# A mixture-of-experts layer hands its results to the next layer: rows scattered by token, or blocks written by slot and gathered by token

## The chip, the cores and the metric

The kernel runs on one core of one Trainium2 chip. The core has five engines that run their own instruction streams in order and meet at semaphores: PE (TensorE, the matrix multiplier; PEld is its weight load), DVE (VectorE), ACT (ScalarE), POOL (GpSimd) and SP (SyncE, which here only issues transfers). Sixteen DMA engines move data between main memory and the on-chip memories. SBUF is the working memory, with 128 partitions; PSUM takes the matmuls' results.

The metric is device time in microseconds (us) of one execution. Eight runs of the kernel before have a median of 2263.39 us, from 2252.53 to 2265.82.

## What is computed

The input x has 4 x 1024 tokens of 128 values. Six layers follow, each with a layer norm in front and added to x. What matters here is the third, the second mixture, and the fourth behind it.

```
x = x + 0.5 * moe(layernorm(x))        # 8 experts, 2 per token
x = x + mamba(layernorm(x))            # scan over time
x = x + 0.5 * moe(layernorm(x))        # the same weights: the "second mixture"
x = x + 0.5 * soft_moe(layernorm(x))   # 64 experts x 32 slots
x = x + gla(layernorm(x))              # gated linear attention
x = x + 0.5 * soft_moe(layernorm(x))
```

The mixture, cut to what matters (T = 4096 tokens, E = 8, K = 2, each expert has cap = 1024 slots):

```python
gates_k, idx_k = top_k(softmax(xt @ wg), K); gates_k /= gates_k.sum(-1)
loc   = position of the choice among all choices of its expert
valid = loc < cap
disp[idx_k, loc] = xt                       # tokens to slots
out   = relu(disp @ w1 + b1) @ w2 + b2      # per expert
y     = sum over k of gates_k * valid * out[idx_k, loc]   # slots back to tokens
```

The soft mixture takes logits = x @ phi.T + phi_b, a softmax over the 32 slots of each expert for the dispatch (its weighted sums over all tokens, X_tilde, are normalised and go through one matrix per expert), and a softmax over the 64 experts for the way back.

## The kernel before

The 4096 tokens are 32 tiles of 128; x stays in SBUF for the whole kernel (P = 128, NT = 32, D = 128). The 8192 slots of the mixture are NSB = 64 blocks of 128 (NSLOT = 8192).

**Routing, `slots`.** From the router's masks it works out each choice's slot (L307 to L320; a choice that finds its expert full gets a gate of 0). A one-hot matmul inverts this: for every slot the row of its token, in `src` (L373), and the row of its choice among the K x T = 8192 choices, in `dest` (L372). An empty slot gets a spare row of its own behind them (L364 to L366). `mamba_layer` comes in front of it, and the framework orders what lies between.

**Experts, `moe_experts`.** A loop over 16 blocks of 512 slots, with the order on PE, DVE, ACT and POOL as written by hand. Per block: four gathers by `src` on POOL (L402), each of 128 rows of 512 bytes from the normalised x in main memory; four transposes (L420) into dT (L422); eight passes for the hidden layer (L430, ACT's relu L434); 32 passes for the output (L444); `eo` = output + b2 on DVE (L449). Then four scatters by `dest` on POOL (L408) write eo's rows into `y2_d`, one row for each choice. Gathers run four blocks ahead in 20 buffers; eo has four buffers. In the last blocks, where there is nothing to gather, a small memset (L472) stands between scatters.

**Back to tokens, `combine`.** `bring` reads y2_d for four tiles in two plain transfers on SP (L488). `pieces` scales the first choice by its gate on ACT (L499), scales the second and adds x on DVE (L491), adds both (L509), and takes the layer norm's sums (L122, L123, L126 in `ln_sums` and `ln_eps`), root on POOL (L136) and shift on DVE (L143). It is a generator: each `yield` ends what one step of its user takes.

**First soft layer, `soft_bounded`.** It runs in the branch that was taken (`bounded`). Again the order on the four engines is written by hand. The dispatch loop has NK = 64 steps, two for each tile of tokens. Step k emits, in this order:

- one yield of `pieces` (eight of them make a group of four tiles),
- `logits(k)`: four passes (L980), and the minimum of the negated logits on DVE (L984); `expo(k)`: the exponential on ACT (L989),
- in the first four of each eight steps, `norm`: one tile of the next group, normalised on ACT (L198); in the fifth `turn` and `take`: four transposes (L966) and their copy to xT (L971). `turn` takes one of the two PSUM buffers that the logits use,
- `total(k-1)`: sums (L996) and reciprocal (L997) on DVE; `weigh(k-1)`: the product on POOL (L1001),
- `spread(k-3)`: four passes (L1012).

In front of the loop stand the pieces of the first group, its norm and turn, and the pieces of the second group. Before that, POOL sets rows of xT to 1 (L946). Behind the dispatch come the experts' part and the way back, which use the 14 buffers of the pool `lp` for their tiles L.

Of the kernel before, what the change touches and what calls it, by code (L numbers as in the profile page):

```python
# [69 lines left out]
def macaron_kernel(ctx: ExitStack, tc: tile.TileContext, a: dict, out: bass.AP):  # L70
# [132 lines left out]
    def moe_routes(tag, tp):  # L203
# [92 lines left out]
        def slots(src, dest, gate):  # L296
            with ExitStack() as s1:
# [31 lines left out]
                )  # L329
                hl_i = sp.tile([P, 2, C], I32, name="hl_i")  # L330
# [33 lines left out]
                none = sp.tile([P, NSB], F32, name="none")  # L364
                nc.vector.tensor_scalar(none, inv[:, 1, :], 0.0, None, ALU.is_equal)
                nc.vector.tensor_tensor(none, none, spare, ALU.mult)  # L366
# [5 lines left out]
                nc.vector.scalar_tensor_tensor(dest, row, -1.0, none, ALU.add, ALU.add)  # L372
                nc.vector.tensor_scalar(src, dest, T - 1, None, ALU.bitwise_and)  # L373
# [15 lines left out]
    def moe_experts(w1, w2, b2, tag, xn_d, src, dest):  # L389

        with ExitStack() as s1:
# [6 lines left out]
            spacer = wk.tile([P, 1], F32, name="spacer")  # L398

# [56 lines left out]
            with tc.manual_schedule(engines=ENGINES):  # L456
                for c in range(AHEAD * 4):
                    gather(c)
                turn(0)
                turn(1)  # L460
                hidden(0)
                for blk in range(NBLK + 1):
                    if blk + 2 < NBLK:
                        turn(blk + 2)
                    if blk + 1 < NBLK:
                        hidden(blk + 1)
                    for i in range(4):
                        c = (blk + AHEAD) * 4 + i
                        if c < NSB:
                            gather(c)  # L470
                        elif blk > 0:
                            nc.gpsimd.memset(spacer, 0.0)  # L472
                        if blk > 0:
                            scatter((blk - 1) * 4 + i)
                    if blk < NBLK:
                        output(blk)

    def combine(gate, ln, n=2, tag=None):
# [47 lines left out]
        return bring, pieces  # L526

# [394 lines left out]
    def soft_bounded(phiN, phiM, pbc, ew, eb, tag, ln, first=None, rest=None, after=None, last=False, yp=None):  # L922
# [12 lines left out]
        with ExitStack() as s:  # L935
# [223 lines left out]
            with tc.manual_schedule(engines=ENGINES):  # L1159
                if first:  # L1160
                    bring, pieces = first
                    bring(0, yp)
                    bring(4, yp)
                    run(pieces(0, yp))
# [4 lines left out]
                if first:  # L1169
                    run(pieces(4, yp))  # L1170
                else:
                    pieces = rest
                others = (_ for j in range(8, NT, 4) for _ in pieces(j, yp))
                for k in range(NK + CS * NB + XL + 3):
                    next(others, None)
                    if k < NK:
                        logits(k)
                        expo(k)
                        g, r = divmod(k, 8)
                        if 4 * (g + 1) < NT:  # L1180
                            if r < 4:
                                norm(4 * (g + 1) + r)
                            elif r == 4:
                                turn(g + 1)
                                take(g + 1)
                        elif r == 4:
                            maxima(0, NT - 4)
# [11 lines left out]
                    if 0 <= k - 1 < NK:  # L1199
                        total(k - 1)  # L1200
                        weigh(k - 1)
                    if 0 <= k - LAG < NK:
                        spread(k - LAG)
# [473 lines left out]
    dest = const.tile([P, NSB], I32, name="dest")  # L1677
    for j in range(0, NT, 4):
        ln_group(lns[0], j)

    with tc.tile_pool(name="moewa", bufs=1) as wpool:
        weights = moe_weights(wpool)
        with tc.tile_pool(name="rtmpa", bufs=1) as tp:
            route = moe_routes("a", tp)
            with (
                tc.tile_pool(name="rxa", bufs=4) as xp,
                tc.tile_pool(name="rpsa", bufs=2, space=PSUM) as ps,
            ):
                for j in range(0, NT, 4):
                    run(route.tiles(j, lns[0], nc.scalar, xp, ps))  # L1690
                    if j % 8 == 4:
                        route.top_two(j - 4, 8)
            route.slots(src, dest, gates[0])
        moe_experts(*weights, "a", route.xn_d, src, dest)
# [3 lines left out]
    with tc.tile_pool(name="rtmpb", bufs=1, side="right") as tp:  # L1698
# [5 lines left out]
        route.slots(src, dest, gates[1])  # L1704
# [12 lines left out]
    moe_experts(*weights, "b", route.xn_d, src, dest)  # L1717
    wpool.close()

    def behind_soft(soft):  # L1720
        gla_layer(lns[4], lns[5])
        ln_root(lns[5], 0, 8)
        soft("b", lns[5], rest=lambda j, _: ln_pieces(lns[5], j), last=True)
# [5 lines left out]
    with tc.If(bounded > 0) as cmp:  # L1729
        def soft(*a_, **k_):  # L1730
            soft_bounded(phiN, phiM, pbc, ew, eb, *a_, **k_)
        with tc.tile_pool(name="yb", bufs=2) as yp:
            soft("a", lns[3], combine(gates[1], lns[3]), after=after, yp=yp)
        behind_soft(soft)
    with cmp.Else():
        def soft(*a_, **k_):
            rest = k_.pop("rest", None)
            if rest:
                for j in range(8, NT, 4):
                    run(rest(j, None))  # L1740
            soft_layer(phiN, ew, eb, *a_, **k_)
        nc.scalar.activation(phiN, phiN, AF.Copy, scale=-1.0)
        with tc.tile_pool(name="yc", bufs=2) as yp:
            bring, pieces = combine(gates[1], lns[3])
            bring(0, yp)
            bring(4, yp)
            for j in range(0, NT, 4):
                run(pieces(j, yp))
# [75 lines left out]
```

## Time and profile before

The profiled execution took 2262.53 us, with a span of 2260.8 us; the mean granted clock of PE was 0.931.

| stretch, us from the span's start | length | PE busy | DVE | ACT | POOL | granted PE clock |
|---|---|---|---|---|---|---|
| experts of the second mixture, 881 to 1052 | 171.0 | 128.6 | 22.4 | 45.9 | 127.1 | 0.92 |
| dispatch, start, 1062 to 1075 | 13.0 | 9.6 | 8.7 | 7.6 | 1.1 | 0.71 |
| dispatch, eight steps, 1132.2 to 1160.8 | 28.6 | 26.9 | 24.4 | 10.9 | 16.6 | 1.00 |
| dispatch of the second soft layer, eight steps, 1839.3 to 1867.8 | 28.5 | 28.1 | 24.0 | 10.9 | 16.2 | 1.00 |

Each row is one stretch of the windows view: how long each engine was busy in it. The busy times of engines overlap, and a busy engine need not be the one that sets the end. The second soft layer has no pieces of a mixture, only those of its layer norm.

From the page's groups:

```profile
L1001 POOL TENSOR_TENSOR dm<-ex,sm 128x1024 f32<-128x1024 f32 x128 | 247.4, 1933 | 217.4 <-DVE sm L997 110.0
L408 POOL DMA_INDIRECT y_d<-eo,dest x128 | 125.7, 982 | 42.3 <-issue 25.0
```

A group's line gives line, engine and operation, the tiles written and read, shapes and count; then the busy time in us and the mean of one in ns; then how long the engine was idle just before them, and what ended most of it. L408 counts both mixtures, 64 scatters in each.

### The profile page before, as it was taken

To read this page: it belongs to the slowest core of one execution; us is meant where nothing else is said; L and a number is where in the kernel's file an instruction comes from. 1 tells how busy PE (TensorE), PEld (TensorE's weight loads), DVE (VectorE), ACT (ScalarE), POOL (GpSimd) and SP (SyncE) were. 2 spreads that over 40 slices of the span, in tenths; PEclk is the share of its full clock that TensorE was granted. 3 is DMA by queue.
4 is the path that set the end of the run, shared out by engine and by line. 5 is a ranking of instruction groups with operands and counts; after the bars stand their busy time and mean duration, and the time that the engine had idled before them with its cause. 6 is when DMAs were issued, how large, how long until landed. Compare 5 with 4: busy or idle time off the path is not lost. (4 is left out here: it accounts for less than half of the span.)

```text
span 2260.8 us, 18041 instructions
## 1 busy us (share of the span) xinstructions
PE 1913.5 (85%) x5889; PEld 890.4 (39%) x5889; DVE 1400.4 (62%) x1852; ACT 957.4 (42%) x1613; POOL 1407.3 (62%) x923
## 2 busy tenths in 40 slices
PE   5688668888888773975999989998888899989998
PEld 3466323333333232653344444443232344434443
DVE  4411578887788864112888745555877788744444
ACT  3222376677766642322334333332543333333331
POOL 2677368888888874676555556663444455556663
PEclk9999779999999895998999999999987899999999
DMA  7111333223223315112000000000000000000000
GB/s 252 32 52 51 111 122 116 99 102 118 100 91 120 102 39 201 46 52 70 19 19 0 1 1 1 0 0 6 0 1 0 1 0 1 0 1 5 10 10 15
DMA packets 63678, 111.23 MB, mean 49 GB/s; under 512 B 8000, under 2 KB 41424, under 8 KB 58582
## 3 DMA queue, kind: packets, MB, share of 16 engines
q1 hardware_dynamic: 49286, 83.46, 11.0%
q0 software_dynamic: 8192, 16.79, 2.5%
q10 hardware_dynamic: 6098, 9.75, 1.3%
q8 instruction: 48, 0.79, 0.1%
q14 instruction: 54, 0.43, 0.1%
HBM read 90.53 MB, written 19.44 MB: 49 GB/s over the span
## 5 line engine op out<-in xcount | busy, mean ns | idle before, releaser
L1001 POOL TENSOR_TENSOR dm<-ex,sm 128x1024 f32<-128x1024 f32 x128 | 247.4, 1933 | 217.4 <-DVE sm L997 110.0
L748 POOL TENSOR_TENSOR hc<-hst,Cs 128x1024 f32<-128x1024 f32 x128 | 292.5, 2294 | 53.5 <-DVE hst L732 29.2
L763 PE MATMUL py<-hc,ident 128*128 128x512 f32 x512 | 275.6, 666 | 49.3 <-POOL hc L748 49.3
L1109 POOL TENSOR_TENSOR acc<-acc,L 128x1024 f32<-128x1024 f32 x96 | 225.9, 2353 | 116.0 <-ACT L L1101 115.3
L1101 ACT ACTIVATE L<-pl,pbc 128x512 f32<-128x512 f32 x256 | 161.9, 683 | 284.2 <-PE pl L1091 273.7
L989 ACT ACTIVATE ex<-l,nmh 128x1024 f32<-128x1024 f32 x128 | 142.6, 1114 | 291.8 <-DVE nmh L984 274.6
L980 PE MATMUL l<-phiT,xT 128*128 128x512 f32 x512 | 248.3, 610 | 19.6 <-ACT ex L989 16.3
L1091 PE MATMUL pl<-xT,phiM 128*128 128x512 f32 x512 | 243.5, 600 | 0.1
L1012 PE MATMUL px<-dm,xn 128*128 128x512 f32 x512 | 241.4, 594 | 1.1 <-POOL dm L1001 1.1
L1135 PE MATMUL py<-L,yt 128*128 128x512 f32 x512 | 238.4, 593 | 4.4 <-DVE L L1125 4.4
L722 ACT ACTIVATE dA<-delta,A 128x512 f32<-128x512 f32 x256 | 177.3, 719 | 69.0 <-DVE hst L732 64.0
L984 DVE TENSOR_REDUCE nmh<-l 128x1 f32<-128x1024 f32 x128 | 156.1, 1220 | 80.6 <-PE l L980 80.0
L434 ACT ACTIVATE hT<-ph,cols 128x512 f32<-128x512 f32 x128 | 87.9, 687 | 217.9 <-PE ph L430 217.9
L763 PEld LDWEIGHTS py<-hc,ident 128*128 128x128 f32 x512 | 94.4, 200 | 197.9 <-issue 106.8
L714 POOL TENSOR_TENSOR dBu<-du,Bs 128x1024 f32<-128x1024 f32 x80 | 170.6, 2134 | 0.5 <-DVE nmr L143 0.5
L732 DVE TENSOR_TENSOR_SCAN hst<-dA,carry,dBu 128x512 f32<-128x512 f32 x128 | 155.5, 1264 | 23.9 <-POOL dBu L714 19.6
L732 DVE TENSOR_TENSOR_SCAN hst<-dA,dBu 128x512 f32<-128x512 f32 x128 | 147.6, 1204 | 24.4 <-POOL dBu L714 18.6
L980 PEld LDWEIGHTS l<-phiT,xT 128*128 128x128 f32 x512 | 97.8, 194 | 151.3 <-issue 116.9
L996 DVE TENSOR_REDUCE sm<-ex 128x32 f32<-128x1024 f32 x128 | 154.6, 1208 | 0.0
L408 POOL DMA_INDIRECT y_d<-eo,dest x128 | 125.7, 982 | 42.3 <-issue 25.0
L1125 DVE TENSOR_TENSOR L<-L,rd 128x1024 f32<-128x1024 f32 x128 | 147.1, 1212 | 0.1
L1135 PEld LDWEIGHTS py<-L,yt 128*128 128x128 f32 x512 | 96.8, 190 | 127.3 <-issue 116.9
(258 smaller groups left out, 2895.6 us busy)
## 6 DMA issues: line engine op xcount, KB each, us to landing
Cs<-bc_d SPq DMA_DIRECT2D x32, 1024.0 KB, 4.7
Bs<-bc_d SPq DMA_DIRECT2D x80, 256.0 KB, 3.1
w<-in_w SPq DMA_DIRECT2D x4, 2048.0 KB
y<-y_d SPq DMA_DIRECT2D x32, 256.0 KB, 2.9
y_d<-zero SPq DMA_DIRECT2D x1, 4096.0 KB
ew<-in_ew ACTq DMA_DIRECT2D x1, 4096.0 KB
x<-in_x SPq DMA_DIRECT2D x8, 256.0 KB, 8.1
xn_da<-xr ACTq DMA_DIRECT2D x8, 256.0 KB, 13.5
```

The costliest lines, as they stand in the source:

```text
L714: eng.tensor_tensor(dBu, r["du"], r.pop(("B", n)).unsqueeze(2).to_broadcast([P, HB, NC]), ALU.mult,)
L722: nc.scalar.activation(dA, r["delta"][:, :, c], AF.Exp, scale=A[:, c * DS + n : c * DS + n + 1],)
L732: nc.vector.tensor_tensor_scan(hst[:, :, c], r.pop(("dA", n, c)), dBu[:, :, c], 0.0 if h == 0 else carry[b][:, c, n : n + 1], ALU.mult, AL ...
L748: nc.gpsimd.tensor_tensor(hc, r.pop(("h", n)), Cs.unsqueeze(2).to_broadcast([P, HB, NC]), ALU.mult)
L763: nc.tensor.matmul(r["py"][:, c, :], ident, hc[:, :, c], start=False, stop=(n == DS - 1))
L980: nc.tensor.matmul(l[:, q * 512 : (q + 1) * 512], xT[:, j * P : (j + 1) * P], phiN[:, o : o + 512], start=True, stop=True,)
L1001: nc.gpsimd.tensor_tensor(dms[k], exs.pop(k), sms.pop(k).unsqueeze(2).to_broadcast([P, NG, PS]), ALU.mult,)
L1012: nc.tensor.matmul(px[hf * 2 + q], xns[j // 4][:, j % 4, :], dmf[:, q * 512 : (q + 1) * 512], start=(j == 0), stop=(j == NT - 1),)
L1091: nc.tensor.matmul(pl[:, i, :], phiM[:, (2 * c + i) * P : (2 * c + i + 1) * P], xT[:, t * TB : (t + 1) * TB], start=True, stop=True,)
L1101: nc.scalar.activation(L[:, i, :], pl[:, i, :], AF.Exp, bias=pbc[:, 2 * c + i : 2 * c + i + 1], scale=-1.0,)
L1109: nc.gpsimd.tensor_tensor(accs[t], accs[t], L, ALU.add)
L1135: nc.tensor.matmul(pys[t], yt[:, 2 * c + i, :], L[:, i, :], start=(c + i == 0), stop=(c == CS - 1 and i == 1),)
```

## The change

In the second mixture only, scatters are left out. Each finished eo block is written by one plain transfer on SP into `ys_d`, a table in main memory with one row for each slot. `slots` keeps every choice's slot in `place` (clipped to the table) instead of working out `dest`. In place of `combine`, `collect` brings the results back: 64 gathers on POOL, one for each of the two choices of each of the 32 tiles, each of 128 rows of `ys_d` by `place`. The tiles y that they fill come from the pool `lp`.

The first soft layer issues 12 gathers in front of its loop, takes the first group through scale, add, statistics and root, issues four more, and then one in each of the first 48 steps, behind `weigh`. The pieces of a group are placed by hand in the steps of the group before it: scale in the third step, add in the fourth, statistics and root in the fifth, minus in the seventh. `norm` moves to the seventh and eighth steps, two tiles in each, and `turn` and `take` to the eighth. The layer norms of the second group are no longer in front of the loop. The first mixture and the second soft layer keep their order.

```diff
+                if place is not None:
+                    nc.vector.tensor_scalar(place, slot, float(NSLOT - 1), None, ALU.min)
...
+                    row_i = sp.tile([P, NSB], I32, name="row_i")
+                    nc.vector.tensor_scalar(row_i, row, -1.0, 0.0, ALU.add, ALU.max)
+                    nc.vector.tensor_scalar(src, row_i, T - 1, None, ALU.bitwise_and)
...
-                        elif blk > 0:
+                        elif blk > 0 and dest is not None:
                             nc.gpsimd.memset(spacer, 0.0)
-                        if blk > 0:
+                        if blk > 0 and dest is not None:
                             scatter((blk - 1) * 4 + i)
                     if blk < NBLK:
                         output(blk)
+                        if dest is None:
+                            c = blk * 4
+                            nc.sync.dma_start(out=ys_v[:, c : c + 4, :], in_=eos[blk])
...
+    def collect(gate, ln, ys_d, place):
+        ys = {}
+        def gather(n, pool):
+            if n < K * NT:
+                j, k = divmod(n, K)
+                g, i = divmod(j, 4)
+                if n % (4 * K) == 0:
+                    ys[g] = pool.tile([P, K, 4, D], F32, name="y", tag="L")
+                c = k * NT + j
+                nc.gpsimd.indirect_dma_start(
+                    out=ys[g][:, k, i, :], out_offset=None, in_=ys_d,
+                    in_offset=bass.IndirectOffsetOnAxis(ap=place[:, c : c + 1], axis=0),
+                )
+        def scale(g):
+            for i in range(4):
+                nc.scalar.activation(
+                    ys[g][:, 0, i, :], ys[g][:, 0, i, :], AF.Copy,
+                    scale=gate[:, 0, g * 4 + i : g * 4 + i + 1],
+                )
+        def add(g):
+            y = ys.pop(g)
+            x4 = x[:, g * 4 : g * 4 + 4, :]
+            for i in range(4):
+                nc.vector.scalar_tensor_tensor(
+                    y[:, 1, i, :], y[:, 1, i, :], gate[:, 1, g * 4 + i : g * 4 + i + 1],
+                    x4[:, i, :], ALU.mult, ALU.add,
+                )
+            nc.vector.tensor_tensor(x4, y[:, 0, :, :], y[:, 1, :, :], ALU.add)
+        return SimpleNamespace(
+            gather=gather, scale=scale, add=add, stats=lambda g: ln_stats(ln, g * 4),
+            root=lambda g: ln_pow(ln, g * 4), minus=lambda g: ln_minus(ln, g * 4),
+        )
...
                 if first:
-                    bring, pieces = first
-                    bring(0, yp)
-                    bring(4, yp)
-                    run(pieces(0, yp))
+                    for n in range(12):
+                        first.gather(n, lp)
+                    first.scale(0)
+                    first.add(0)
+                    first.stats(0)
+                    first.root(0)
+                    for n in range(12, 16):
+                        first.gather(n, lp)
+                    first.minus(0)
...
                 for k in range(NK + CS * NB + XL + 3):
                     next(others, None)
+                    g, r = divmod(k, 8)
+                    g += 1
+                    new = 4 * g < NT
+                    if first and new:
+                        if r == 3:
+                            first.add(g)
+                        elif r == 4:
+                            first.stats(g)
+                        elif r == 6:
+                            first.minus(g)
                     if k < NK:
                         logits(k)
                         expo(k)
...
+                        n0 = 6 if first else 0
+                        if new and n0 <= r < n0 + (2 if first else 4):
+                            for i in range(2) if first else (r,):
+                                norm(4 * g + (2 * (r - n0) if first else 0) + i)
+                        if new and r == (7 if first else 4):
+                            turn(g)
+                            take(g)
+                        if first and new and r == 2:
+                            first.scale(g)
...
                     if 0 <= k - 1 < NK:
                         total(k - 1)
                         weigh(k - 1)
+                    if first and k < NK:
+                        first.gather(16 + k, lp)
+                        if new and r == 4:
+                            first.root(g)
                     if 0 <= k - LAG < NK:
                         spread(k - LAG)
...
-        with tc.tile_pool(name="yb", bufs=2) as yp:
-            soft("a", lns[3], combine(gates[1], lns[3]), after=after, yp=yp)
+        soft("a", lns[3], collect(gates[1], lns[3], ys_d, place), after=after)
```

## The prediction

> **What bounds the kernel now.** All times are us. I read the page first, then the timeline of the stretches the edit touches: the second mixture's experts (881 to 1052), the hand-over to the first soft layer (1045 to 1065) and that layer's dispatch loop (1065 to 1300). In the experts the fence below, PE's timeline, shows two early blocks and two late ones.
>
> ```profile
> 924.96 3.73 PE L444 MATMUL po<-w,hT 128*128 128x128 f32 x32
> 932.41 3.73 PE L444 MATMUL po<-w,hT 128*128 128x128 f32 x32
> ...
> 954.65 0.33 PE L420 MATMUL pt<-ident,g 128*128 128x128 f32 x1 [2.21 <-DMA g<-xn_db,src]
> ...
> 958.26 3.73 PE L444 MATMUL po<-w,hT 128*128 128x128 f32 x32
> ...
> 964.87 0.33 PE L420 MATMUL pt<-ident,g 128*128 128x128 f32 x1 [2.32 <-DMA g<-xn_db,src]
> ```
>
> The first two are 7.45 apart: PE's own work sets the pace. Later blocks are 964.87 - 954.65 = 10.2 apart and PE waits 2.2 for a gather in each: POOL, which alternates one gather and one scatter, cannot keep up. So POOL bounds the experts, PE the dispatch. One group of the dispatch is eight steps, and it has one stall, at its fifth step:
>
> ```profile
> 1143.55 1.29 DVE L126 TENSOR_SCALAR rstd<-mv 128x4 f32<-128x4 f32 x1
> ...
> 1146.05 1.11 ACT L989 ACTIVATE ex<-l,nmh 128x1024 f32<-128x1024 f32 x1 [3.23 <-DVE nmh L984]
> ...
> 1147.22 1.98 PE L980 MATMUL l<-phiT,xT 128*128 128x512 f32 x4 [1.66 <-ACT ex L989]
> ```
>
> A step is 3.43 of PE (four L980 and four L1012 passes). A group is 8 x 3.43 + 0.44 for the transposes + the stall = 29.83, the distance of L1001 at 1132.59 and 1162.42. The last group with transposes has no layer-norm pieces and takes 28.54 (1251.90 to 1280.44).
>
> **Two behaviours the sum needs.** First, DVE and POOL block each other where both read two operands from SBUF (timelines of the dispatch, of the mamba layer and of the first soft layer's second half):
>
> ```profile
> 1132.37 0.51 DVE L491 SCALAR_TENSOR_TENSOR y<-y,gate,x 128x128 f32<-128x128 f32 x2
> ...
> 1132.59 2.06 POOL L1001 TENSOR_TENSOR dm<-ex,sm 128x1024 f32<-128x1024 f32 x1 [1.37 <-ACT xn L198]
> ```
>
> ```profile
> 485.96 1.23 DVE L673 SCALAR_TENSOR_TENSOR w<-w,e 128x1024 f32<-128x1024 f32 x1 [0.55 <-ACT l L671]
> 486.06 6.18 POOL L748 TENSOR_TENSOR hc<-hst,Cs 128x1024 f32<-128x1024 f32 x2
> 487.23 3.02 DVE L674 TENSOR_TENSOR l<-l,w 128x1024 f32<-128x1024 f32 x1
> ...
> 1395.51 1.02 POOL L136 TENSOR_TENSOR rstd<-rstd,half_t 128x4 f32<-128x4 f32 x1 [1.10 <-DVE rstd L126]
> 1396.50 2.34 POOL L1109 TENSOR_TENSOR acc<-acc,L 128x1024 f32<-128x1024 f32 x1
> 1396.56 2.30 DVE L143 SCALAR_TENSOR_TENSOR nmr<-mv,rstd 128x4 f32<-128x4 f32 x1 [1.13 <-POOL rstd L136]
> ```
>
> L491's pair took 0.51 and went ahead, while L1001, started 0.22 after it, took 2.06 instead of 1.91. L674 needs 1.22 alone (its shortest) and took 3.02: POOL, waiting, got in between two DVE instructions. L143 needs 0.16 alone and took 2.30: the POOL operation queued behind the root started first. Second, PE is slow after idling:
>
> ```profile
> 1085.86 3.20 PE L980 MATMUL l<-phiT,xT 128*128 128x512 f32 x4 [2.29 <-ACT ex L989]
> 1088.85 2.40 PE L1012 MATMUL px<-dm,xn 128*128 128x512 f32 x4
> ```
>
> After 2.29 idle these two groups took 3.20 and 2.40 instead of 1.88, and the windows view grants 0.87 and 0.63 around them; after the stalls of 1.66 the clock stayed at 1.00.
>
> **The change, part by part.**
>
> *Slots.* One DVE operation more (`place`, as L331: 0.20), two of 0.23 (L365, L366) fewer on the way to `src`: taken as 0, bounds -0.5 to +0.5.
>
> *Experts.* Scatters leave POOL: gathers alone are 1.25 apart (887.66, 888.90), four in 5.0, less than PE's 7.45. So all blocks run at 7.44. Output 13 starts at 910.08 + 13 x 7.44 = 1006.8 instead of 1029.98; the two after it do not wait for gathers now and keep their length. **-23.2.** The 16 transfers on SP (0.37 to issue) hide behind PE; without that cover only the last counts, and it is in the next part.
>
> *Hand-over.* From the last eo (E) to the first logits it was 1045.02 to 1065.02 = 20.0. After: the write lands 2.3 later (as out<-x; xn_db<-xr, nearer to traffic, took 5.5), POOL starts 0.3 after that (as 914.82 after eo), so gathers from E+2.6. POOL issues 12, then the root: 11 x 1.25 + 0.97 = 14.7, root at E+17.3. The data is no later: gather 7 starts at E+11.35, lands 2.5 on, then one scaled add, the sum, the statistics and the hand to POOL, 0.29 + 0.73 + 1.9 + 0.15, E+16.9. Root to first logits was 1065.02 - 1060.80 = 4.2. Together 21.5: **+1.5**, bounds +1 (the data chain alone, E+16.9) to +8 (3.2 more for the write, 3.5 more if the 3.51 of L946 must wait for E and is not covered by idle POOL). First logits thus 21.7 earlier.
>
> *A group of dispatch with collect.* Count from the group's first logits. One step of DVE is 2.66 (L984 to L996 1.14, to L997 1.25, to the next 0.27); L984 can start 1.91 after its logits; L1001 starts 0.5 after L997; ex starts 1.32 after L984 and lets PE go 1.17 later.
> - Steps 0 to 2 are on time: L984 at 1.91, 5.34, 8.77; L997 at 11.16, DVE free at 11.43; L1001 starts at 11.66.
> - Step 3, add: four scaled adds and a sum, 1.6 alone. Two go (to 11.94), as in the row at 1132.37; POOL then takes the port until 13.7 (L1001, 1.91), the other two and the sum end at 14.8. L984 at 14.8 instead of 12.2, L1001 at 17.7 to 19.6.
> - Step 4, statistics: four pairs at 0.40, 17.46 to 19.06; eps (L126) waits for L1001's end, 19.6, as the 1.29 above. L984 at 19.55, ex at 20.9, PE waits until 22.0. L1001 22.4 to 24.35, then the gather (0.25 + 0.97, as between scatter and gather) to 25.6, then the root (1.01) to 26.6.
> - Step 6, minus: DVE is free at 24.9, behind it queue L984 and all of PE's next logits; it waits for the root and then, as at 1396.56, for the L1001 that starts at 26.57: 28.5. L984 28.4.
> - Step 7: L984 at 31.06, ex 32.4; the last two norms stand behind ex on ACT (1.01 and 0.41 later, 0.48 long), end 34.3; the transposes behind them on PE end 34.4, and in front of L1012 and the next logits. Next group's logits at 36.2.
> - PE has idled from 27.9 to 34.5 with four small transposes in it. One slow window costs at most 3.2 + 2.4 - 2 x 1.88 = 1.84; by where the window falls I take 1.4 of 0 to 2.2.
>
> Group: **37.6**, instead of 29.83: +7.8. Without locks add ends at 13.06, minus at 24.9, and the same walk gives 32.8 (+1.2 clock). Both ends are kept; I take 37.6, as its rows are of these very lines.
>
> Five full groups: 5 x 7.8 = 39.0. The last (no gathers, root ends 25.4, minus 27.3, next logits 35.0 + 1.4 = 36.4 against 28.54): +7.9. The first: 36.1 + 1.4 = 37.5 against 1097.96 - 1065.02 = 32.94: +4.5. **Sum of the dispatch: +51.4.**
>
> *POOL's gathers in the steps* fit: 1.91 + 0.25 + 0.97 = 3.13 a step under 3.43, so POOL does not set the pace; if a gather took 1.9, the root would be 0.95 later in six groups, +6. Their landing (2.5) is three steps ahead of use: 0. SP's y transfers (1053.03 and later) are gone: their waits are in the hand-over. The eight y tiles take eight of the 14 L buffers; the seventh L is the first to need one again, long after the adds: 0.
>
> A DVE copy that can lock the port does not hold a POOL transfer:
>
> ```profile
> 1045.57 0.97 POOL L408 DMA_INDIRECT y_d<-eo,dest  x1 [0.19 <-issue]
> 1045.63 0.23 DVE L919 COPY smod<-sm 128x128 f32<-128x128 f32 x1
> ```
>
> The Trainium skill (SBUF — State Buffer, The "DVE blocks DMA" trap) speaks against that: descriptors of a POOL transfer stand still while DVE runs a two-port operation. The row shows 0.97, as without the copy; by the page each eps could hold a gather by eps's own 0.17, some 1 in all, by the row 0.
>
> On the clock, the Trainium skill (TensorE: Matmul & The Clock Gate, What's actually happening) asks for a whole idle window of about 3.4 before half speed; the rows show it after 2.29. Both put a 6.6 gap on the slow side; by the page's window an estimate is 1.7 for each of seven stalls, 11.9 instead of my 9.8.
>
> **Sum.** -23.2 + 1.5 + 51.4 = +29.7. The profiled execution took 2262.53 around a span of 2260.8; the median of the eight runs is 2263.39, 0.9 above it. Span after about 2290.5, median **2293**.
>
> **Rivals.**
> 1. *The port does not bite* (other side): place, step 3 and step 6; DVE's add and minus run at once. For it: STT and L1001 at 1132.37 cost only 0.15. Against: 3.02 and 2.30 above. Price: a group of 32.8, so five +3.0, last 31.6 - 28.54 = +3.1, first -0.3, -21.7: -3.9, 2259.5; with the clock loss 7 x 1.4 it is +5.9, 2269. It decides from 21.7 / 7 = 3.1 a group: below that the change is not slower.
> 2. *The late norms are covered too*: groups stay at 29.83, only the experts' gain shows: 2263.39 - 21.7 = 2241.7. Against: ACT runs norms behind ex in program order, and PE has nothing before the transposes.
> 3. *Gathers are dear between POOL's compute* (1.9 and more): +6 for roots, and with 3 a gather POOL's step is 1.91 + 0.25 + 3 = 5.2, a group 41.3 + 1.0 in place of 36.2: 5 x 6 more, 2305 to 2323. Against: scatter after memset in the tail keeps 0.97.
> 4. *The experts do not speed up* (SP's writes hold eo's four buffers, or gathers are late for another reason): half the gain lost, 2305. Against: 7.45 a block leaves a 2.3 landing room.
>
> **Numbers.** My forecast 0.66, own range 2278 to 2303; rival 1 0.14, rival 2 0.04, rival 3 0.09, rival 4 0.07. 0.3% (6.8, about what this kernel's runs can tell from no change) is 2256.6 to 2270.2: rival 1 gives 0.03 faster, 0.07 same, 0.04 slower. Slower 0.86, same 0.07, faster 0.07. The range for 8 in 10 reaches to rival 1 with clock loss and to rival 4: 2266 to 2306.
>
> **What would show it.** Right: outputs 7.44 apart to the end and no gather wait on PE; L1001 groups 36 to 38 apart; L143 of about 1.9 right after the root; scaled adds with one of about 2; L966 waiting for xn, and slow L980 after it. Wrong: groups under 33, or L1001 waiting for POOL's own gathers.

## The result, and the profile after

The kernel after takes 2292.22 us (median of 7 runs, 2291.05 to 2295.93); the kernel before, with all its runs, 2260.27 (2252.53 to 2265.82). The ratio is 1.0145, 95% interval 1.013 to 1.016: 32 us slower. The forecast was 2293. The profiled execution took 2294.17 around a span of 2292.4, at a mean granted clock of PE of 0.922 (0.931 before).

The difference of the two spans, 31.6, is found again stage by stage in the two timelines. E is the end of the last `eo`, S0 the first logits of the soft layer, S56 the first logits of its last group of four tiles:

| stage | before | after | difference |
|---|---|---|---|
| start to the end of the mamba layer (not touched by the change) | 838.57 | 842.03 | +3.5 |
| from there to the first gather of the experts (slots) | 42.68 | 41.73 | -1.0 |
| first gather to first output | 28.83 | 27.40 | -1.4 |
| first output to E (experts) | 134.94 | 111.80 | -23.1 |
| E to S0 (hand-over) | 20.00 | 22.82 | +2.8 |
| S0 to S56 (seven groups of dispatch) | 210.62 | 262.55 | +51.9 |
| S56 to the end | 985.2 | 984.1 | -1.1 |

PE's timeline of the second mixture's experts, after (start, length, engine, line, operation, tiles, shapes, count, and in brackets the idle time before it):

```profile
940.93 3.73 PE L456 MATMUL po<-w,hT 128*128 128x128 f32 x32
944.50 0.60 PE L432 MATMUL pt<-ident,g 128*128 128x128 f32 x4
944.94 3.60 PE L442 MATMUL ph<-dT,w 128*128 128x512 f32 x8
948.37 3.73 PE L456 MATMUL po<-w,hT 128*128 128x128 f32 x32
...
955.82 3.73 PE L456 MATMUL po<-w,hT 128*128 128x128 f32 x32
```

No bracket is left, so PE waits for no gather, and the outputs stay 7.44 apart to the end. This answers to the two rows of the prediction in which the transposes waited 2.21 and 2.32 for a gather.

One group of the dispatch, from its first logits at 1158.77 (timeline of all engines, cut to the rows in which time is lost):

```profile
1170.21 2.76 DVE L571 SCALAR_TENSOR_TENSOR y<-y,gate,x 128x128 f32<-128x128 f32 x4
1170.44 2.06 POOL L1055 TENSOR_TENSOR dm<-ex,sm 128x1024 f32<-128x1024 f32 x1 [0.39 <-DVE sm L1051]
...
1173.08 0.69 DVE L575 TENSOR_TENSOR x<-y 128x512 f32<-128x512 f32 x1
1173.68 1.22 DVE L1038 TENSOR_REDUCE nmh<-l 128x1 f32<-128x1024 f32 x1
...
1184.34 1.05 POOL L136 TENSOR_TENSOR rstd<-rstd,half_t 128x4 f32<-128x4 f32 x1
...
1185.38 1.90 POOL L1055 TENSOR_TENSOR dm<-ex,sm 128x1024 f32<-128x1024 f32 x1
1185.43 1.88 DVE L143 SCALAR_TENSOR_TENSOR nmr<-mv,rstd 128x4 f32<-128x4 f32 x1 [1.71 <-POOL rstd L136]
...
1187.23 1.21 DVE L1038 TENSOR_REDUCE nmh<-l 128x1 f32<-128x1024 f32 x1
...
1192.67 0.86 PE L1020 MATMUL pt<-ident,xn 128*128 128x128 f32 x2 [1.73 <-ACT xn L198]
...
1193.32 3.20 PE L1066 MATMUL px<-dm,xn 128*128 128x512 f32 x4
```

Read it from the top. The four scaled adds need 0.35 each in the hand-over, where POOL runs no weigh beside them; here they take 2.76, because the weigh L1055, which writes dm, gets in after two of them and the third takes 2.00. The reduction behind them, L1038, starts 14.9 after the group's logits instead of 12.2. The minus, L143, works on 128 x 4 numbers and takes 1.88, as long as the weigh that started 0.05 before it. Everything on DVE stands behind it, so the seventh step's reduction comes 28.46 after the group's logits. The last transposes wait for the norms, and the matmuls behind them take 3.20 instead of 1.88. The next logits start 37.6 after the first. All seven minus operations in the loop take 1.88 or 1.89 (the one in the hand-over, with no weigh beside it, 0.16), and the seven groups 36.7 to 37.7.

The windows view of this group has 31.52 busy of 37.58 for PE and 24.38 for POOL: neither engine is full. The time lies in waits and in the slow matmuls behind them (granted clock 0.91 over the group).

### The profile page after: what moved, and what is told of

Same layout as the page of the kernel before. It is cut to its first block, busy times and chain, and to the rows that moved or that the text cites. A ratio compares the mean times of both kernels' runs of the same rounds, so it can differ in the third digit from the quotient of the medians.

```text
span 2292.4 us, 18006 instructions
## 1 busy us (share of the span) xinstructions
PE 1928.1 (84%) x5889; PEld 891.8 (39%) x5889; DVE 1424.6 (62%) x1851; ACT 958.5 (42%) x1613; POOL 1400.1 (61%) x903
## 5 line engine op out<-in xcount | busy, mean ns | idle before, releaser
L1055 POOL TENSOR_TENSOR dm<-ex,sm 128x1024 f32<-128x1024 f32 x128 | 245.4, 1918 | 216.7 <-DVE sm L1051 129.4
L1066 PE MATMUL px<-dm,xn 128*128 128x512 f32 x512 | 252.1, 616 | 6.8 <-POOL dm L1055 6.8
L1038 DVE TENSOR_REDUCE nmh<-l 128x1 f32<-128x1024 f32 x128 | 155.1, 1212 | 105.7 <-PE l L1034 105.7
L786 DVE TENSOR_TENSOR_SCAN hst<-dA,carry,dBu 128x512 f32<-128x512 f32 x128 | 155.5, 1265 | 23.9 <-POOL dBu L768 19.6
L1066 PEld LDWEIGHTS px<-dm,xn 128*128 128x128 f32 x512 | 98.9, 199 | 131.1 <-issue 110.8
```

The source lines that it names most:

```text
L786: nc.vector.tensor_tensor_scan(hst[:, :, c], r.pop(("dA", n, c)), dBu[:, :, c], 0.0 if h == 0 else carry[b][:, c, n : n + 1], ALU.mult, AL ...
L1038: nc.vector.tensor_reduce(nmh[:, j, hf : hf + 1], l, AX.X, ALU.min)
L1055: nc.gpsimd.tensor_tensor(dms[k], exs.pop(k), sms.pop(k).unsqueeze(2).to_broadcast([P, NG, PS]), ALU.mult,)
L1066: nc.tensor.matmul(px[hf * 2 + q], xns[j // 4][:, j % 4, :], dmf[:, q * 512 : (q + 1) * 512], start=(j == 0), stop=(j == NT - 1),)
```

## The experiments

The kernels ran in four sets. In the first the kernel before took 2261.09, close to the 2260.27 of the result above. The other sets were on chips where it took 2306.85 and more; the last experiment deals with that. There, times are compared as ratios to the kernel before and by the length of a group, which is the same on all these chips. In kernels that split the add, line numbers behind it are 10 higher (L1038 is L1048, L1055 is L1065, L1020 is L1030).

**The root in front of the weigh.** It takes the weigh away from where the minus waits, and POOL's weigh and gather from in front of the root.

```diff
                         total(k - 1)
+                        if first and k < NK and new and r == 4:
+                            first.root(g)
                         weigh(k - 1)
                     if first and k < NK:
                         first.gather(16 + k, lp)
-                        if new and r == 4:
-                            first.root(g)
```

> The root (L136 in the kernel after) stands on POOL in front of the fifth step's weigh instead of behind that weigh and its gather. Theory (the port and POOL's queue delay the minus): in the group from 1158.77 the root starts near 1179.9 instead of 1184.34, no weigh stands behind it when it ends, so the minus (L143) takes 0.16 instead of 1.88, runs right behind the reciprocal at 1183.75, and the next logits of the group come about 3.3 earlier: group 34.3 instead of 37.6, seven times, about 2269 in all (2263 if the slow matmuls go too). Rival 1 (the port does not bite; the minus is 1.88 for some other reason): the minus stays at 1.9 wherever the root stands, and only the wait shrinks: at most 1.6 a group, 2281. A theory in which the minus bounds nothing: 2292.

It took 2271.59, ratio 1.0047 (1.0031 to 1.0063): 20.6 less than the kernel after, where 23 was expected. Its timeline, in the group from 1144.41:

```profile
1165.26 1.05 POOL L136 TENSOR_TENSOR rstd<-rstd,half_t 128x4 f32<-128x4 f32 x1
...
1166.92 1.91 POOL L1055 TENSOR_TENSOR dm<-ex,sm 128x1024 f32<-128x1024 f32 x1 [0.62 <-DVE sm L1051]
...
1169.28 0.10 DVE L143 SCALAR_TENSOR_TENSOR nmr<-mv,rstd 128x4 f32<-128x4 f32 x1
1169.29 1.21 DVE L1038 TENSOR_REDUCE nmh<-l 128x1 f32<-128x1024 f32 x1
1170.05 1.93 POOL L1055 TENSOR_TENSOR dm<-ex,sm 128x1024 f32<-128x1024 f32 x1
```

The root starts 20.85 after the group's logits instead of 25.57. The weigh behind it is over when the minus is due, and the next one has not begun: the minus takes 0.10. The reduction comes at 24.88, as the theory had it (25.0). Groups are 33.3 to 35.9, since slow matmuls stand behind the transposes in some groups and not in others, and S0 to S56 is 242.2, so 20.3 less than after. Rival 1 is out: the length of the minus follows the place of the weigh.

The Trainium skill (SBUF — State Buffer, Who interferes with whom) states that a DVE instruction with two SBUF inputs and a POOL instruction that reads SBUF lock each other out for a whole instruction, and that issue order decides who waits. The 1.88 behind a weigh and the 0.10 without one agree with it.

**The scaled adds in pairs.**

```diff
                         if r == 3:
-                            first.add(g)
+                            first.plus(g)
+                        elif r == 1 or r == 2:
+                            first.scaled(g, 2 * (r - 1), 2)
...
-                        if first and new and r == 2:
+                        if first and new and r == 0:
                             first.scale(g)
```

`scaled` is the loop of `add` over two tiles, `plus` its sum.

> The four scaled adds go in two pairs into the second and third steps (the scaling goes to the first), and only the sum stays in the fourth. Theory: a pair slips in front of the weigh, as in the kernel before (0.51 to 0.58), so no scaled add takes 2.0 and the fourth step's first reduction starts 12.2 after the group's logits instead of 14.9; the eps still waits for a weigh; the root starts about 2.0 earlier and the minus still takes 1.9 behind it. Group 35.6, 2279 in all (bounds 2273 to 2288). Rival (the adds' place costs nothing, since the root and minus wait for POOL in any case): no change, 2292.

It took 2274.36, ratio 1.0055 (1.0033 to 1.0076): 17.9 less than after; S0 to S56 is 14.3 less. Its timeline, group from 1153.61:

```profile
1158.19 0.51 DVE L571 SCALAR_TENSOR_TENSOR y<-y,gate,x 128x128 f32<-128x128 f32 x2
1158.42 2.05 POOL L1065 TENSOR_TENSOR dm<-ex,sm 128x1024 f32<-128x1024 f32 x1 [5.21 <-DVE sm L1061]
...
1165.83 1.23 DVE L1048 TENSOR_REDUCE nmh<-l 128x1 f32<-128x1024 f32 x1
...
1176.50 1.05 POOL L136 TENSOR_TENSOR rstd<-rstd,half_t 128x4 f32<-128x4 f32 x1
1177.54 1.90 POOL L1065 TENSOR_TENSOR dm<-ex,sm 128x1024 f32<-128x1024 f32 x1
1177.59 1.88 DVE L143 SCALAR_TENSOR_TENSOR nmr<-mv,rstd 128x4 f32<-128x4 f32 x1 [1.71 <-POOL rstd L136]
```

A pair goes in front of the weigh, at 0.51, and the weigh is 0.15 longer for it. The fourth step's reduction starts at 12.22, on time. The minus still meets its weigh and takes 1.88, but the root came 2.7 earlier, so the group is 34.6 to 36.3 (35.5 on average, 35.6 expected). The rival, that the adds' place costs nothing, is out.

**The norms earlier.**

```diff
-                        if new and n0 <= r < n0 + (2 if first else 4):
-                            for i in range(2) if first else (r,):
-                                norm(4 * g + (2 * (r - n0) if first else 0) + i)
+                        if new and n0 <= r < n0 + (1 if first else 4):
+                            for i in range(4) if first else (r,):
+                                norm(4 * g + i)
```

> All four norms stand behind the seventh step's exponential instead of two behind the seventh's and two behind the eighth's. Theory: the last transposes no longer wait for the eighth step's exponential; they end about 1.4 earlier, the next logits start 1.3 earlier: group 36.3, 2283 in all, and down to 2274 if the shorter idle stretch on PE also removes the slow matmuls behind it. Rival 2 (the norms were covered; the minus alone sets the end of the group): no change, 2292.

It took 2277.62, ratio 1.0074 (1.0047 to 1.0102): 14.6 less, more than the 9 of the first estimate and within its bounds. Groups are 35.1 to 36.6, the last 33.1. Timeline and windows of the group from 1151.64 (windows: stretch, its length, busy time of PE, weight loads, DVE, ACT and POOL with their counts, granted PE clock, DMA share, GB/s):

```profile
1183.27 1.64 ACT L198 ACTIVATE xn<-x,nmr,rstd 128x128 f32<-128x128 f32 x4
...
1183.80 1.63 PE L1020 MATMUL pt<-ident,xn 128*128 128x128 f32 x4 [3.14 <-ACT xn L198]
...
1185.23 3.00 PE L1066 MATMUL px<-dm,xn 128*128 128x512 f32 x4
```

```profile
1183.80:1185.20 1.40, 1.34 (x4) 0.75 (x5) 1.40 (x2) 1.40 (x4) 1.37 (x1) 0.59 0.00 0
1185.20:1188.00 2.80, 2.80 (x5) 1.23 (x5) 1.03 (x2) 1.24 (x2) 2.63 (x3) 0.59 0.09 23
```

The transposes now wait once, for the first norms, and not a second time behind the eighth step's exponential. PE still idles 3.14 before them and runs at 0.59 of its clock during and behind them. Rival 2, that the norms are covered, is out.

**PE kept busy.**

```diff
-                        logits(k)
+                        logits(k, 2 if first and new and r == 7 else 1)
...
-                for q in range(2):
+                for q in (0, 1) * times:
```

> The eighth step's logits are computed twice into the same tile (the same values), which keeps PE busy for 1.88 of the stretch in which it idles. Theory of the clock (PE is slow after idling over 2): the stretch shrinks to gaps under 2, L1066 behind the transposes takes 1.88 to 2.4 instead of 3.20, and a group gets 0.8 to 1.3 shorter although PE does more: 2283 to 2287. Rival (the clock does not follow that idle, or the 3.20 is a wait for something else): the same, 2292, or later by up to 1.9 a group if the doubled logits delay the reduction.

It took 2289.92, ratio 1.0124 (1.0098 to 1.0151); groups are 36.4 to 37.7, S0 to S56 0.8 less. PE's timeline:

```profile
1182.17 3.60 PE L1034 MATMUL l<-phiT,xT 128*128 128x512 f32 x8
1187.18 0.71 PE L1020 MATMUL pt<-ident,xn 128*128 128x128 f32 x2 [1.42 <-ACT xn L198]
1189.78 0.86 PE L1020 MATMUL pt<-ident,xn 128*128 128x128 f32 x2 [1.88 <-ACT xn L198]
1190.43 3.17 PE L1066 MATMUL px<-dm,xn 128*128 128x512 f32 x4
```

The expectation failed in its size. The doubled logits cost nothing, so PE had that time to spare, but L1066 stays at 3.17, behind gaps of 1.42 and 1.88 with two short transposes between them. It is not the length of one gap that decides. In the experts of the kernel before PE has eight gaps of 2.13 to 2.39, the 2.21 and 2.32 of the prediction among them, and the windows view grants 1.00 over the whole stretch from 910.1 to 1045.0; in its dispatch PE was slow after 2.29. The windows view of this run shows what the added work did:

```profile
1186.20:1189.60 3.40, 0.66 (x2) 0.28 (x2) 3.33 (x5) 2.69 (x5) 2.24 (x2) 1.00 0.07 19
1189.60:1193.00 3.40, 3.23 (x6) 1.47 (x7) 0.04 (x1) 1.09 (x3) 3.22 (x3) 0.50 0.06 19
```

In the first 3.4 PE is busy for 0.66, and in the next 3.4, in which L1066 runs, it has half its clock. In the kernel after the same group has 0.50 and 0.51 in two such stretches, from 1189.2 to 1196.0. So the 1.7 of work halved the slow stretch, but the half that is left is the one that holds L1066.

**Root first and split adds together.** Both edits above.

> The root in front of the fifth step's weigh and the scaled adds in pairs, together. Theory (each stall stands in line behind the one before): with the adds split, the run with the split alone keeps its logits 3.43 apart up to the eighth step, and only the minus (1.88, behind root and weigh) holds its seventh step's reduction by 3.3; with the root first that goes too, so all reductions are on time. What is left is the last two norms and transposes behind the eighth step's exponential. Group 31 to 32 (8 x 3.43 + some 3.5 for norms and transposes, with or without slow matmuls), 2245 to 2253 in all. If the two edits only overlap (both remove the same wait): a group of 34, 2268.

2303.65 where the kernel before took 2306.85, ratio 0.9976 (0.9961 to 0.999). Groups are 31.1 to 33.3, where each alone had 34.6 and 35.5 on average. S0 to S56 is 223.5, so 39.1 less than after, where the two alone saved 20.3 and 14.3. The two do not overlap; each takes its own stall away. The ratio lies a little above the 0.993 to 0.997 that the expected times make.

**And the norms early.** All three edits.

> The same with all four norms behind the seventh step's exponential. Theory: nothing in a group waits any more but PE for its own work: 8 x 3.43 + 1.6 for four transposes, group 28.0 to 29.0, 2225 to 2232 in all, below the kernel before by 1.3 to 1.6%. If PE stays slow behind the transposes for some other reason than idling: 1.4 more in each group, 2235 to 2242.

2282.52, ratio 0.989 (0.987 to 0.9909). Groups are 28.6 to 29.1, and no slow matmul is left in the dispatch but at its start: the first two groups of logits, behind the idle time of the hand-over, take 3.75 and 2.17. The last row of the expectation, PE slow for some other reason than idling, is out with that. The ratio of 0.989 lies above the 0.985 to 0.987 that the times of the expectation make; the groups are as long as expected, so that difference lies outside them.

**And the ones of xT written by DVE.**

```diff
-            nc.gpsimd.memset(xT[96:P, :], 1.0)
+            nc.vector.memset(xT[96:P, :], 1.0)
```

The hand-over of the kernel after first, from the last `eo`; its fence is the timeline:

```profile
1022.27 0.69 DVE L461 TENSOR_TENSOR eo<-po,b 128x512 f32<-128x512 f32 x1 [2.88 <-PE po L456]
1022.99 0.36 SPq L491 DMA_DIRECT2D ys_d<-eo  x1
...
1023.16 3.51 POOL L1000 MEMSET xT<- 32x4096 f32 x1 [51.10 <-PE po L456]
1023.48 3.27 DVE L973 COPY smod<-sm 128x128 f32<-128x128 f32 x1
1026.82 0.95 POOL L555 DMA_INDIRECT y<-ys_d,place  x1 [0.16 <-issue]
```

POOL has been idle for 51.10, yet the memset runs after PE's last output, and the first gather stands behind it on POOL. The bracket names that output as what it waited for.

> The same with the ones of xT written by DVE instead of POOL. Theory (the 3.51 of L1000, which waits for PE's last output, holds POOL's first gather): the first gather of the hand-over comes at the landing of the last write, 2.5 to 2.7 after the last eo instead of 3.86, and the first logits come 21.5 after it instead of 22.8; in all 1.3 less than the kernel with three edits. Otherwise: no change in the hand-over, or a longer one if DVE's fill holds POOL.

```profile
1062.30 0.69 DVE L461 TENSOR_TENSOR eo<-po,b 128x512 f32<-128x512 f32 x1 [2.88 <-PE po L456]
...
1063.98 3.47 DVE L1010 MEMSET xT<- 32x4096 f32 x1 [0.99 <-DVE eo L461]
1066.06 0.95 POOL L555 DMA_INDIRECT y<-ys_d,place  x1 [53.95 <-DMA ys_d<-eo]
```

Now the gather waits for the write, as it should, and starts 3.07 after E instead of 3.86. From E to the first logits it is 21.93, against 22.86 in the kernel with three edits: 0.93 less, of 1.3 expected. In all 2275.98, ratio 0.9865 (0.9847 to 0.9884). That is 6.5 less than with three edits, but the runs of the two kernels overlap (2274.22 to 2280.13, and 2273.63 to 2287.83), and S0 to S56 is no shorter (203.4 against 202.8); only the 0.93 is shown.

**Transposes and copy in front of the eighth step's exponential.**

```diff
                         logits(k)
+                        if first and new and r == 7:
+                            turn(g)
+                            take(g)
                         expo(k)
...
-                        if new and r == (7 if first else 4):
+                        if new and not first and r == 4:
                             turn(g)
                             take(g)
```

> The kernel with the four edits, and the transposes and the copy into xT stand in front of the eighth step's exponential instead of behind it. In the kernel with four edits the next logits wait for that copy (0.33 at the start of a group, group 29.02). Theory: the copy comes 1.3 earlier, PE then runs through: group 28.4 to 28.6, seven times, 3 to 4 less than with four edits, ratio to the kernel before 0.985. If the exponential, now behind the copy, holds the reductions of the next group: no gain, 0.9865.

2270.46 (2259.2 to 2281.37) where the kernel before took 2312.47, ratio 0.9807 (0.9782 to 0.9833). This is the fastest version. Groups are 28.4 (the first 28.8), as expected, against 29.83 in the kernel before, and S0 to S56 is 4.0 less than with four edits. The rival, that the exponential would hold the reductions, is out. The ratio fell by more than that, from 0.9865, but in this set the kernel before took 2312.47 instead of 2306.85. Timeline and windows:

```profile
1257.83 1.11 PE L1030 MATMUL pt<-ident,xn 128*128 128x128 f32 x4
...
1258.78 1.88 PE L1076 MATMUL px<-dm,xn 128*128 128x512 f32 x4
1258.98 0.59 ACT L1035 COPY xT<-pt 127x512 f32<-127x512 f32 x1 [0.42 <-PE pt L1030]
...
1260.49 1.88 PE L1044 MATMUL l<-phiT,xT 128*128 128x512 f32 x4
```

```profile
1203.65:1232.08 28.43, 28.35 (x70) 12.56 (x69) 24.72 (x40) 12.11 (x18) 24.84 (x18) 1.00 0.07 19
```

PE is busy for 28.35 of 28.43 and bounds the dispatch at last. POOL carries as much as in the kernel after (24.84, gathers and all): its load was not the trouble, but the order in which its operations met DVE's, and the place of the norms on ACT.

**What set the experts' pace: gathers added.** In the kernel after, a second gather of rows of the same table into a tile that nobody reads, where a scatter stood before.

```diff
+                        elif blk > 0 and c < NSB:
+                            c0 = (blk - 1) * 4 + i
+                            extra = xgp.tile([P, D], F32, name="extra")
+                            nc.gpsimd.indirect_dma_start(
+                                out=extra, out_offset=None, in_=xn_d,
+                                in_offset=bass.IndirectOffsetOnAxis(
+                                    ap=src[:, c0 : c0 + 1], axis=0),
+                            )
```

> The kernel after, where POOL issues a second gather (into a tile that nobody reads) at each place in the experts where the kernel before issued a scatter beside a gather; 44 in all. Theory (POOL's issue rate, two indirect transfers of 1.25 for each tile, set the experts' pace): outputs 7.44 apart at first and then 10.0 apart; the last gather is issued at 883.8 + 107 x 1.25 = 1017.5, the output that needs it starts near 1021 instead of 1007.9, and the whole takes 13 more: 2305. Rival (the scatters were slow because of what they wrote or waited for): outputs stay 7.44 apart, 2292.

2387.29, ratio 1.0343 (1.0318 to 1.0368), far more than expected. POOL issued a pair every 2.50 where it had nothing to wait for, as the theory had it. But PE's matmuls came one by one in stretches of this stage, with up to 2.53 between them for which no wait is named (more on that below), and this run can't tell how much of its loss POOL's pace made.

**What set the experts' pace: POOL's time alone.** In the kernel after, a fill at the same 44 places.

```diff
+            fill = wk.tile([P, 1600], F32, name="fill", bufs=1)
...
+                        elif blk > 0 and c < NSB:
+                            nc.gpsimd.memset(fill, 0.0)
```

> The kernel after, where POOL fills a scratch tile (128 x 1600, by the rate of L1000 about 1.4) at each of the 44 places where the kernel before issued a scatter beside a gather: the same time on POOL, no transfer. Theory (POOL's time set the pace of the experts): gather and fill together take 2.55; the first 20 gathers are out 25 after the first, the last one 43 x 2.55 later, 18 to 19 later than PE's own pace needs after it has landed: outputs 10.2 apart in the second half, the last eo some 16 later, ratio to the kernel before 1.021 to 1.022 instead of 1.0145. Rival (the scatters' transfers, not POOL's time, held the gathers): outputs 7.44 apart, 1.0145.

2336.53, ratio 1.0108 (1.0089 to 1.0126). By its time the theory would fall. The timeline says more (POOL, then PE):

```profile
1036.45 0.95 POOL L415 DMA_INDIRECT g<-xn_db,src  x1 [0.16 <-issue]
1037.40 1.45 POOL L489 MEMSET fill<- 128x1600 f32 x1
1039.01 0.95 POOL L415 DMA_INDIRECT g<-xn_db,src  x1 [0.17 <-issue]
```

```profile
1028.16 0.84 PE L433 MATMUL pt<-ident,g 128*128 128x128 f32 x3
1031.83 0.48 PE L433 MATMUL pt<-ident,g 128*128 128x128 f32 x1 [2.83 <-DMA g<-xn_db,src]
```

Gather and fill are 2.57 apart, and PE waits for gathers again, as in the kernel before. From the first output (930.69) to E (1060.91) it is 130.2, against 111.8 in the kernel after on the first chip: +18.4, where 16 was expected. The waits for gathers make 11.3 of it, and the matmuls behind the two longest waits are slow (L443 takes 5.97 and 6.49 instead of 3.61), which makes most of the rest; this stage of this run shows no other new wait on PE. The outputs were not 10.2 apart each time but 7.44 to 14.38, so that the sum comes close to 16 is in part luck. The ratio does not show the loss, because on this chip the kernel after needed 127.7 for the same stage, for another reason:

**The kernel after and the kernel before, unchanged, on the later chips.**

> The kernel after, unchanged, beside the kernel before on the chip of this set: 1.0145 times the kernel before, whatever the time of that one is here.

> The kernel before, unchanged, with a profile from the chip of the later sets, if this run gets that chip: there the kernel after shows stretches (in both mixtures' experts) in which PE gets its matmuls one by one with 1.0 to 2.5 between them for which the profile names no wait. If the 50 by which the kernel before is longer on that chip comes from the same stretches, its trace shows them too, in the first and second experts, and groups of 29.83 in the dispatch as ever. If not, the time was lost elsewhere.

The kernel after had 2335.28 against 2312.47, ratio 1.0101 (1.0079 to 1.0123), not the 1.0145 expected. The kernel before had 2313.81, on a third chip. PE's timeline in the experts of the kernel after on the later chip:

```profile
934.09 3.06 PE L456 MATMUL po<-w,hT 128*128 128x128 f32 x26
939.15 0.27 PE L456 MATMUL po<-w,hT 128*128 128x128 f32 x1 [2.00 <-issue]
941.26 0.27 PE L456 MATMUL po<-w,hT 128*128 128x128 f32 x1 [1.83 <-issue]
```

PE gets single matmuls with 2 between them, and "issue" means that the profile names no wait. In the first set no such rows are seen. Here the waits view counts 36.0 + 6.7 + 2.0 = 44.7 us of them in the kernel after and 47.7 + 5.3 + 2.0 = 55.0 in the kernel before, in both mixtures' experts. The kernel after is 38.8 later at E (1061.79 against 1022.96), the kernel before 48.4 at S0 (1113.38 against 1065.02); behind that both run nearly as on the first chip, with groups of 37.6 and 29.83. The difference, 9.6, is about the 0.4% between the ratios 1.0145 and 1.0101, though kernel before and kernel after were profiled on different chips here. What holds PE's instructions there stays open, and so does why the run with the fills has no such rows in the second mixture.

So part of the gain of the last version against the kernel before also comes from these stalls. Against the kernel after in the same set it is 64.8 (2335.28 to 2270.46); S0 to S56 took 199.3 in it and 262.55 in the kernel after, 63.2 less, and the hand-over gives some 1 more. By these differences an estimate for the first chip is 2292.2 - 64 = 2228, 1.4% below the kernel before; it was not run there.

## Why the prediction was right

**Experts, -23.2.** Measured -23.1. POOL's pace was the cause: the fills, which take POOL's time and transfer nothing, brought back the pairs at 2.57 and waits for gathers, 11.3 in sum, and with slow matmuls 18.4 of time. This rests on one trace, held against the kernel after on another chip.

**Slots, 0 (bounds -0.5 to +0.5).** Measured -1.0, outside. The two timelines show where: L365 no longer stands in front of the copy to `row` (0.26), and on DVE a memset (0.48) that stood between `row` and `dest` now runs ahead of them, which brings the next operation 0.76 closer. The prediction counted the first and not the second.

**Hand-over, +1.5.** Measured +2.8, within the bounds of 1 to 8. The term that failed is "gathers from E+2.6": they came from E+3.86. I had priced the memset L1000 as covered by idle POOL unless it must wait for E; it did wait for PE's last output, and its other end was in the range only. Moving it to DVE gave 0.9 back; the write itself holds the gather until 3.07.

**The group, 37.6.** Measured 37.6 to 37.7 for the five full ones. The walk held step by step; the forecast stands first, the measured time in brackets: fourth step's reduction 14.8 (14.9), fifth's 19.55 (19.6), root 26.6 at its end (26.6), minus until 28.5 (28.5), eighth's reduction 31.06 (31.1), transposes until 34.4 (34.5 to the next matmul). The first group was 37.5 (37.7), the last 36.4 (36.7); the sum +51.4 (+51.9). Each of its three stalls was then shown by taking it away: the minus behind the weigh, the adds behind the weigh, and the norms behind the exponential. The three do not add: they saved 20.3, 14.3 and 13.9 of S0 to S56 alone, 48.5 in sum, and 59.7 together. Behind the first two groups of logits, slow matmuls (over 2.1 for four) are still found in the dispatch with each edit alone and with the first two together, and none with all three, which fits the surplus.

**The clock, 1.4.** The matmuls behind the transposes took 3.20 instead of 1.88 in the group shown, so 1.3, and 3.02 to 3.62 in the seven groups: 9.8 lost in sum, the 7 x 1.4 of the forecast; the other estimate there, 11.9, was too high. The size was right, but the picture behind it, slow after one gap of over 2, was wrong. The gaps of 2.21 and 2.32 in the prediction's own rows spoke against it, and the run with the doubled logits showed two gaps under 2 that were enough. The Trainium skill (TensorE: Matmul & The Clock Gate, What's actually happening) has a window of activity that runs by itself instead; that run's rows, where 3.4 with 0.66 of work in it were followed by half the clock, speak for a count over a stretch and against a count of one gap.

**Rivals.** The port that does not bite: out by the minus of 0.10 against 1.88. Taking away the lock between DVE and POOL without moving an operation was not tried. Norms covered: out. Dear gathers: out, L555 took 0.98 between the weighs. The experts not faster: out by the outputs 7.44 apart. Some of the close agreement is luck: this execution was 3.5 longer before it reached the changed code, which no term of the sum has, and the slots, the way to the first output and the end gave 3.5 back.

## What to carry to other kernels

A change that frees one engine by moving work into another stage should be costed where the work lands: here 23 saved were paid for with 52, though no engine was full there. A tiny operation of one engine that shares a port with another can cost as much as the large one that it meets (here 1.88 instead of 0.10), so place it where the other engine's operation is over, and look at which operation stands next in that queue when its operand comes. Taken away one at a time, the three stalls were worth 48.5, and together 59.7: the slow matmuls behind the transposes were gone only with the last gap.

## What was not expected of the hardware

- A POOL operation that only writes holds a DVE copy: the smod copy took 3.27 beside the memset L1000 (3.51) and 0.22 in the kernel where DVE writes those ones itself.
- DVE writes the 32 x 4096 ones in 3.47, POOL in 3.51; and the gathers that POOL issued during DVE's fill took 0.95, as elsewhere.
- On two chips PE got its matmuls one by one in stretches of the experts' stages, 44.7 and 55.0 of waiting in all, without a wait that the profile names.
- Two gaps of 1.42 and 1.88 with 0.66 of work between them were followed by half the clock; eight single gaps of 2.13 to 2.39, each between stretches of full work in the experts, were not.
